# Two attention stages of a transformer block: VectorE put into source order in the second, and the weight-sum matmuls issued one step later in the first

## The chip, the cores and the metric

The kernel runs on one core of a Trainium2 chip. The metric is the device time of one execution in microseconds (us); smaller is better. A core has TensorE (PE, matrix products, with a separate weight load PEld), VectorE (DVE), ScalarE (ACT), GpSimd (POOL) and SyncE (SP, which issues most of the DMAs). Each engine executes its own list of instructions in order; engines wait for each other by semaphores.

## The reference, cut to what matters

The input has 4 batches of 512 tokens and 512 channels. Four sublayers follow each other, each with a layer norm in front and a residual sum behind it.

```python
x = x + attn0(layernorm(x))        # 16 heads of 32, rope, rms norm of q and k, causal softmax
x = x + ternary_ffn(layernorm(x))
x = x + selective_scan(layernorm(x))
z = layernorm(x)
h = z + attn1(rmsnorm(z, ln1))     # latent attention, 16 heads of 32, causal softmax
x = x + h + moe(rmsnorm(h, ln2))   # one shared and seven routed experts, top 2
```

Both attentions compute `softmax(q k^T * scale, causal) v` and then a product with an output matrix. In both the sum of the exponentials is divided out only after the product with `v`.

## The kernel before, in words

Tiles have 128 partitions. In both attentions PSUM is divided into two pair buffers, each of two banks (`pair`), and four single banks (`bank`). All names of tiles that come from `pair` share the two buffers (`sc`, `scd`, `pqd`), and all that come from `bank` share the four (`sm`, `av`, `pq`, `tp`, `tpd`, `avd`, `y`, `pl`, ...).

**Order.** The instructions are written in Python loops, and a scheduler (Tile's) then places the instructions of each engine by a model of their durations. `tc.manual_schedule(engines=...)` (L417 and L1457 here) takes the named engines out of this: they keep the order in which the source issues them. In before that is TensorE alone, in both attentions; VectorE, ScalarE, GpSimd and SyncE are placed by the scheduler. It may therefore draw an instruction forward past others of its engine if its inputs are there.

**First attention** (`attend`, L346). For each batch there are 16 steps (g, j): 4 groups of 4 heads, 4 blocks of 128 keys. Scores are kept transposed, with keys on the partitions, so the weights need no transposing, but the sums over keys need a matmul with ones. A step consists of
- `scores` (L361 to L367): 4 matmuls into two `sc` pairs, 2 exponentials on ScalarE into `pt`, and a causal mask on GpSimd (`affine_select`),
- `add` (L385): VectorE adds the weights of the block before to those of this one, so that one matmul with ones gives the running sum,
- `weigh` (L377): 4 matmuls of the weights with `v` into the bank `av`,
- `invert` (L392, L396): 8 matmul instructions with ones into the bank `sm` (the sums of 128 queries, 4 heads), a reciprocal on VectorE, and after the last block the product `oT` (L398).

At loop index m the source issues the scores of step m, the `add` of step m-2, then the fillers `between[m]` (projections of the next batch L284, the output product of the last one L340, transposes, jobs for the ternary weights), then `weigh` of step m-1, then `invert` of step m-2. After the loop two transposes of the next batch follow (`turn_heads`), and then `finish`, which in before adds and inverts the last step.

**Second attention** (L1457 to L1487). One loop over 128 steps plus 4, 32 steps for each batch: 4 head groups, 4 blocks t of 128 queries, 2 pairs of heads. Within a batch, `at` is the number of the step, and this document calls it step 0 to 31. At step m the source issues
- `turn` of step m-3: transposes of the weights on TensorE (L1410) into `tpd`, copied to `ptd` once by VectorE (L1415) and once by ScalarE (L1417),
- `soften` of step m: the scores `scd` (L1387, 4 rows of the array in use), on VectorE the addition of the mask (L1390) and the negative maximum `nm` (L1395), on ScalarE two exponentials `pr` (L1398) with their sums,
- at the ends of groups `widen_sums` (L1441, L1443) and `invert` (L1453, L1455), and in every second step `weigh` (L1428) for two pairs four steps back, with the product `oTd` (L1435) at a group's end,
- as fillers from step 4 a part of `leave(b-1)`: four output products `y` (L1327) with residual sums (L1330, L1331) and squares (L1335) in steps 4 to 7, scaling (L1342) and transposes into `hTr` in steps 8 to 11, then the router,
- and from step 7 a part of `enter(b+1)` (from L1002): statistics of the layer norm (L108, L109) in steps 7 to 10; at step 11 the shift (L150), and in steps 11 to 14 the normalised rows (L155, ScalarE) and their squares (L1015, ScalarE); the inverse root (`ri_rms`: L102 on VectorE, the power L103 on GpSimd) at step 14; from step 15 scaled rows `row_d` (L1028) and their transposes into `hTd` (L132, L133); then the latent projections (L1044, L1062 to L1069) and the rotations.

`enter` for batch 1 runs in batch 0, and so on; batch 3 has none. `leave` for batch 0 runs in batch 1, and so on. The input `x` of all batches is there when the second attention begins.

These are the loops of the two stages around the edit, as the printed functions show in full:

```python
if m > 1:
    add(*steps[m - 2])
for part in between.get(m, ()):
    part()
if m > 0:
    weigh(*steps[m - 1])
if m > 1:
    invert(*steps[m - 2])
```

Of the kernel before, what the change touches and what calls it, by code (L numbers as in the profile page):

```python
# [46 lines left out]
def block_kernel(ctx: ExitStack, tc: tile.TileContext, a: dict, out: bass.AP):  # L47
# [16 lines left out]
    def pair(name):  # L64
        return banks["pair"].tile([P, 2, 512], F32, tag="pair", name=name)

    def bank(name):
        return banks["bank"].tile([P, 512], F32, tag="bank", name=name)
# [95 lines left out]
    with tc.tile_pool(name="a_w", bufs=1) as aw, tc.tile_pool(name="a_1", bufs=1) as a1, tc.tile_pool(  # L164
# [180 lines left out]
        def attend(b, between):  # L345

            qkT, v = turned_qk[b], values[b]
            oT = outs[b] = a1.tile([P, NK, T], F32, tag="oT", name="oT")
            weights, averages, inverses = {}, {}, {}

            def scores(g, j):
                w = T - j * P
                pt = weights[g, j] = a2.tile([P, HG, w], F32, tag=f"pt{j}", name=f"pt{j}", bufs=1)
                both = [pair("sc") for _ in range(2)]
                for i in range(HG):
                    rows = slice(i * D, (i + 1) * D)  # L360
                    nc.tensor.matmul(  # L361
                        both[i // 2][:, i % 2, :w], qkT[rows, NG + g, j * P : (j + 1) * P],
                        qkT[rows, g, j * P :], start=True, stop=True,
                    )
                for i, sc in enumerate(both):
                    nc.scalar.activation(pt[:, 2 * i : 2 * i + 2, :w], sc[:, :, :w], AF.Exp, scale=SCALE)  # L366
                nc.gpsimd.affine_select(  # L367
                    out=pt[:, :, 0:P], in_=pt[:, :, 0:P], compare_op=ALU.is_ge, fill=0.0,
                    base=0, pattern=[[0, HG], [1, P]], channel_multiplier=-1,
                )  # L370

            def weigh(g, j):
                if j == 0:
                    averages[g] = bank("av")
                for i in range(HG):
                    h = g * HG + i
                    nc.tensor.matmul(  # L377
                        averages[g][i * D : (i + 1) * D, j * P :], v[:, j, h * D : (h + 1) * D],
                        weights[g, j][:, i, :], start=j == 0, stop=j == NT - 1,
                    )  # L380

            def add(g, j):
                if j > 0:
                    pt = weights[g, j]
                    nc.vector.tensor_tensor(pt, pt, weights[g, j - 1][:, :, P:], ALU.add)  # L385

            def invert(g, j):
                if j == 0:
                    inverses[g] = a2.tile([P, T], F32, tag="r", name="r", bufs=1)
                sm = bank("sm")  # L390
                for i in range(HG):
                    nc.tensor.matmul(  # L392
                        sm[i * D : (i + 1) * D, :P], ones[:, :D], weights[g, j][:, i, :P],
                        start=True, stop=True,
                    )
                nc.vector.reciprocal(inverses[g][:, j * P : (j + 1) * P], sm[:, :P])  # L396
                if j == NT - 1:
                    nc.vector.tensor_tensor(oT[:, g, :], averages.pop(g), inverses.pop(g), ALU.mult)  # L398

            steps = [(g, j) for g in range(NG) for j in range(NT)]  # L400
            for m in range(len(steps) + 1):
                if m < len(steps):
                    scores(*steps[m])
                if m > 1:
                    add(*steps[m - 2])
                for part in between.get(m, ()):
                    part()
                if m > 0:
                    weigh(*steps[m - 1])
                if m > 1:  # L410
                    invert(*steps[m - 2])
            return lambda: (add(*steps[-1]), invert(*steps[-1]))

        def do(f, *args):
            return lambda: f(*args)
# [1 line left out]
        with tc.manual_schedule(engines={mybir.EngineType.PE}):  # L417
# [39 lines left out]
            for b in range(B):  # L457
# [20 lines left out]
                if b == B - 1:  # L478
                    first_mv = const.tile([P, NT, 2], F32, tag="mv", name="mv")
                    for t in range(NT):  # L480
                        between[9].append(do(statistics, a1, xs[0], t, first_mv))
                finish = attend(b, between)
                if b + 1 < B:
                    turn_heads(b + 1, 2)
# [302 lines left out]
    with tc.tile_pool(name="b_s", bufs=1) as bs, tc.tile_pool(name="b_1", bufs=1) as b1, tc.tile_pool(  # L787
# [79 lines left out]
        with tc.manual_schedule(engines={mybir.EngineType.PE}):  # L867
# [4 lines left out]
            for b in range(B):  # L872
# [10 lines left out]
                def part(n):  # L883
                    if n % 3 == 2 and n > 3 * 4 and b + 1 < B:
                        next(coming, None)
                        if not light[0]:
                            return
                    if n not in (2, 3, 5):
                        light[0] = next(between, False)
# [194 lines left out]
    with tc.tile_pool(name="c_1", bufs=1, reuse_waits="tile") as c1, tc.tile_pool(  # L1084
# [7 lines left out]
        steps = [(b, n, half) for b in range(B) for n in range(NS) for half in range(2)]  # L1092
# [19 lines left out]
        def turn(b, n, half, i):  # L1112
            bu = bank("bu")
            k = 2 * half + i

            nc.tensor.matmul(  # L1116
                bu[:, :P], loaded[b][1][:, 0, k * P : (k + 1) * P], scaled[b, n][0],
                start=True, stop=True,
            )
            for t in range(1, NT):  # L1120
                nc.tensor.transpose(  # L1121
                    bu[:, t * P : (t + 1) * P], scaled[b, n][t][:, k * P : (k + 1) * P], ident
                )
            turned.setdefault((b, n, half), []).append(bu)
# [9 lines left out]
        def weigh(b, n, half):  # L1134
            if half == 0:
                cb = c1.tile([P, T], F32, tag="cb", name="cb", bufs=3)
                nc.sync.dma_start(cb, c_rows[b, n].partition_broadcast(P))
                weighed[b, n] = cb
            hc = c2.tile([P, 2, T], F32, tag="hc", name="hc", bufs=4)
            nc.gpsimd.tensor_tensor(  # L1140
                hc, states.pop((b, n, half)), weighed[b, n].unsqueeze(1).to_broadcast([P, 2, T]), ALU.mult
            )
            states[b, n, half] = hc
# [23 lines left out]
        engines = {getattr(mybir.EngineType, e) for e in ("PE", "DVE", "Activation", "Pool", "SP")}  # L1167
# [142 lines left out]
    with tc.tile_pool(name="d_1", bufs=1) as d1, tc.tile_pool(name="d_2", bufs=2) as d2, tc.tile_pool(  # L1310
# [128 lines left out]
        def widen_sums(b, g):  # L1439
            total = sums.pop((b, g))  # L1440
            nc.vector.reciprocal(total, total)  # L1441
            wides[b, g] = d1.tile([P, T], F32, tag="wide", name="wide")
            nc.scalar.copy(  # L1443
                wides[b, g].rearrange("p (t i d) -> p t i d", t=NT, i=HG),
                total.unsqueeze(3).to_broadcast([P, NT, HG, D]),
            )

        def invert(b, g):

            wide = wides.pop((b, g))  # L1450
            tp = bank("tpr")
            for t in range(NT):
                nc.tensor.transpose(tp[:, t * P : (t + 1) * P], wide[:, t * P : (t + 1) * P], ident)  # L1453
            inverses[b, g] = d1.tile([P, T], F32, tag="inv", name="inv")
            nc.scalar.copy(inverses[b, g], tp)  # L1455

        with tc.manual_schedule(engines={mybir.EngineType.PE}):  # L1457
            for _ in come:
                pass
            left = iter(())  # L1460
            n = len(pairs)
            each = n // B
            for m in range(n + 4):
                b, at = divmod(m, each)
                if 3 <= m < n + 3:
                    turn(*pairs[m - 3])
                if m < n:
                    soften(*pairs[m])
                if 1 <= m < n + 1 and pairs[m - 1][2:] == (NT - 1, 1):
                    widen_sums(*pairs[m - 1][:2])  # L1470
                if 3 <= m < n + 3 and pairs[m - 3][2:] == (NT - 1, 1):
                    invert(*pairs[m - 3][:2])
                if m >= 5 and m % 2 == 1:
                    weigh(*pairs[m - 4][:3])

                if m == (B - 1) * each:
                    fetch_shared()
                if m >= each and at == 3:
                    left = leave(b - 1, outs[b - 1])
                if at >= 4:  # L1480
                    next(left, None)
                if at == 7:
                    come = enter(b + 1, d2) if b + 1 < B else iter(())
                if at >= 7:
                    next(come, None)

            filler = shared(0, d1, "lat")  # L1487
            for _ in range(NK):
                next(filler)
            for _ in range(NT):  # L1490
                next(left)
            for _ in filler:
                pass
            for _ in left:
                pass
# [6 lines left out]
    with tc.tile_pool(name="e_1", bufs=1, reuse_waits="tile") as e1, tc.tile_pool(  # L1502
# [255 lines left out]
        engines = {mybir.EngineType.PE, mybir.EngineType.DVE, mybir.EngineType.Activation}  # L1758
# [64 lines left out]
```

## Time and profile before

| | us |
|---|---|
| median of 3 runs | 1857.02 |
| lowest and highest | 1854.37, 1859.17 |
| the profiled execution | 1858.7 |
| its span, first to last instruction | 1857.0 |
| first attention with its projections | about 55 to 424 of the span |
| ternary feed-forward | 424 to about 740 |
| selective scan | about 740 to 1102 |
| second attention | about 1102 to 1512 |
| experts | 1512 to 1857 |

The mean clock granted to TensorE is 0.98 of full speed. All times of instructions that follow are microseconds from the start of the span of this one profiled execution.

How to read the lines. A row of a stretch has its start and end, its length, then for PE, PEld, DVE, ACT and POOL the busy time and in brackets the number of instructions, then the granted TensorE clock, the share of the DMA engines' time and GB/s (a row asked for TensorE alone has only its busy time in front of the clock). A row of waits reads "engine, tile and line that waited <- engine, tile and line that released it: us in total, times, longest". A row of the timeline has the start, the duration, the engine, line, operation, the tile written and those read, the shapes, the number of instructions drawn together, and in square brackets the idle time of the engine just before it with what ended it.

### The profile page before, as it was taken

What the parts mean: (1) busy time and instruction counts of PE and PEld (TensorE: products, weight loads), DVE (VectorE), ACT (ScalarE), POOL (GpSimd) and SP (SyncE); (2) the same over time, 40 slices, a digit from 0 to 9 for tenths busy, and PEclk for the clock granted to TensorE, in tenths of its full rate; (3) what the DMA queues carried; (4) which work ended last, traced back from release to release, by engine and by line L of the source; (5) the groups of instructions that cost most, each with busy time, mean ns of one, the idle gap of its engine ahead of it and who ended that gap; (6) DMA issues with size and microseconds to landing.
All of it is one profiled execution on the core that took longest, in us unless ns stands there. A gap on an engine that the chain in (4) does not pass through costs nothing.

```text
span 1857.0 us, 27575 instructions
## 1 busy us (share of the span) xinstructions
PE 1740.2 (94%) x10374; PEld 1093.0 (59%) x10374; DVE 1186.6 (64%) x1908; ACT 938.0 (51%) x1940; POOL 581.5 (31%) x383
## 2 busy tenths in 40 slices
PE   7899899989999998989997989999999999999998
PEld 3443344437777676878886875556556554544444
DVE  6577757786655556899887886574766764322222
ACT  2433533332242536889988867576676652111111
POOL 2231313120202021889887860100000000244431
PEclk9999999999999999999999988999999999999999
DMA  7002300102011112333223200000010006455545
GB/s 244 22 1 68 109 1 1 46 1 76 5 40 53 59 56 82 94 92 102 58 73 102 58 28 1 1 24 1 1 35 24 24 24 230 150 91 91 91 79 142
DMA packets 74630, 115.07 MB, mean 62 GB/s; under 512 B 9546, under 2 KB 34762, under 8 KB 73940
## 3 DMA queue, kind: packets, MB, share of 16 engines
q1 hardware_dynamic: 64996, 90.87, 15.4%
q0 software_dynamic: 8656, 20.32, 6.1%
q10 hardware_dynamic: 848, 2.13, 0.3%
q8 instruction: 83, 1.36, 0.3%
q14 instruction: 47, 0.39, 0.1%
HBM read 83.02 MB, written 33.42 MB: 63 GB/s over the span
## 4 chain that ended last, share of the span: by engine, by line
PE 68%; DVE 13%; ACT 11%; issue 3%; DMA 3%; POOL 1%; DVEq 0%; SPq 0%; ACTq 0%; POOLq 0%
PE pgr L1702 7%; PE pg L844 6%; PE pq L284 5%; PE ys L1153 4%; PE yr L1723 4%; PE scd L1387 4%; PE bu L1121 3%; PE y L1327 3%; PE y L862 3%; PE pge L1288 3%; PE tp L132 3%; PE bu L1116 3%; PE y L340 3%; PE tpd L1410 2%; ACT pr L1398 2%
## 5 line engine op out<-in xcount | busy, mean ns | idle before, releaser
L1140 POOL TENSOR_TENSOR hc<-h,cb 128x1024 f32<-128x1024 f32 x128 | 301.1, 2378 | 115.4 <-DVE h L1129 93.7
L1129 DVE TENSOR_TENSOR_SCAN h<-da,bu 128x512 f32<-128x512 f32 x256 | 295.1, 1204 | 28.5 <-PE bu L1121 14.3
L284 PE MATMUL pq<-wqkv,hT 128*128 128x512 f32 x384 | 179.6, 615 | 4.8 <-DVE qk L300 3.6
L1109 ACT ACTIVATE da<-delta_l,am 128x511 f32<-128x511 f32 x256 | 163.4, 709 | 2.1 <-DVE h L1129 2.0
L1398 ACT ACTIVATE pr<-scd,nm 128x128 f32<-128x128 f32 (+3 forms) x256 | 133.3, 530 | 57.6 <-DVE nm L1395 56.7
L844 PE MATMUL pg<-hTh,w 128*128 128x512 f32 (+1 forms) x352 | 145.6, 414 | 1.0 <-ACT hTh L831 0.7
L844 PE MATMUL pg<-hTl,w 128*128 128x512 f32 (+1 forms) x352 | 139.9, 397 | 0.2 <-DVE hTl L832 0.2
L1153 PE MATMUL ys<-ident,hc 128*128 128x128 f32 x1024 | 136.7, 277 | 3.3 <-DVE h L1129 1.7
L1121 PE MATMUL bu<-ident,bu 128*128 128x128 f32 x768 | 132.2, 279 | 6.4 <-ACT bu L1103 6.4
L1702 PE MATMUL pgr<-wgu,gTe 128*128 x304 | 137.1, 593 | 0.0
L1103 ACT ACTIVATE bu<-dxT,bts 128x512 f32<-128x512 f32 x192 | 124.3, 712 | 16.2 <-PE bu L1121 13.3
L284 PEld LDWEIGHTS pq<-wqkv,hT 128*128 128x128 f32 x384 | 71.5, 194 | 97.3 <-issue 91.2
L366 ACT ACTIVATE pt<-sc 128x1024 f32<-128x1024 f32 (+3 forms) x128 | 83.3, 698 | 78.0 <-PE sc L361 72.3
L1387 PE MATMUL scd<-kTd,qTd 32*128 32x512 f32 (+3 forms) x512 | 109.0, 507 | 14.0 <-ACT pr L1398 11.3
L1153 PEld LDWEIGHTS ys<-ident,hc 128*128 128x128 f32 x1024 | 119.0, 143 | 4.3 <-DVE h L1129 1.9
L1116 PE MATMUL bu<-diag_l,dxT 128*128 128x128 f32 x512 | 105.9, 289 | 16.3 <-DVE h L1129 13.3
L367 POOL TENSOR_SCALAR_AFFINE_SELECT pt<-pt 128x512 f32<-128x512 f32 x64 | 56.2, 879 | 179.1 <-ACT pt L366 156.5
L1395 DVE TENSOR_REDUCE nm<-scd 128x2 f32<-128x256 f32 (+3 forms) x128 | 105.0, 821 | 2.8
L1410 PE MATMUL tpd<-ident,pr 128*128 128x128 f32 x640 | 102.6, 290 | 3.5 <-ACT ptd L1417 1.1
L1116 PEld LDWEIGHTS bu<-diag_l,dxT 128*128 128x128 f32 x512 | 82.3, 196 | 40.0 <-DVE h L1129 23.2
L1121 PEld LDWEIGHTS bu<-ident,bu 128*128 128x128 f32 x768 | 95.6, 145 | 9.9 <-ACT bu L1103 9.9
L1709 DVE SCALAR_TENSOR_TENSOR hidr<-pgr,silr 128x256 f32<-128x256 f32 x38 | 16.1, 425 | 130.0 <-ACT silr L1707 130.0
(338 smaller groups left out, 3290.7 us busy)
## 6 DMA issues: line engine op xcount, KB each, us to landing
cb<-c_rows SPq DMA_DIRECT2D x64, 256.0 KB, 3.3
q_w<-in_w2T SPq DMA_DIRECT2D x20, 256.0 KB, 2.8
diag_l<-diags SPq DMA_DIRECT2D x64, 64.0 KB, 2.0
hrows<-h SPq DMA_DIRECT2D x4, 1024.0 KB, 4.3
acc<-x SPq DMA_DIRECT2D x16, 256.0 KB, 2.0
wgu<-in_r_gate SPq DMA_DIRECT2D x7, 512.0 KB, 9.5
wgu<-in_r_up SPq DMA_DIRECT2D x7, 512.0 KB, 10.0
wdn<-in_r_down SPq DMA_DIRECT2D x7, 512.0 KB, 9.3
```

Source lines behind the costliest of these rows:

```text
L284: nc.tensor.matmul(y, inputs_T[b][:, k, t * P : (t + 1) * P], wqkv[:, k, s * C : (s + 1) * C], start=k == 0, stop=k == NK - 1,)
L844: nc.tensor.matmul(pg[:rows, i, :], w[:, k, f * P : f * P + rows], part[:, k, :], start=k + m == 0, stop=k + m == NK,)
L1109: nc.scalar.activation(da[:, k, 1:], delta[:, k, 1:], AF.Exp, scale=am[:, k, n : n + 1])
L1116: nc.tensor.matmul(bu[:, :P], loaded[b][1][:, 0, k * P : (k + 1) * P], scaled[b, n][0], start=True, stop=True,)
L1121: nc.tensor.transpose(bu[:, t * P : (t + 1) * P], scaled[b, n][t][:, k * P : (k + 1) * P], ident)
L1129: nc.vector.tensor_tensor_scan(h[:, i, :], decays[b, n][:, 2 * half + i, :], bu, 0.0, ALU.mult, ALU.add)
L1140: nc.gpsimd.tensor_tensor(hc, states.pop((b, n, half)), weighed[b, n].unsqueeze(1).to_broadcast([P, 2, T]), ALU.mult)
L1153: nc.tensor.matmul(sums[b][t][:, k * P : (k + 1) * P], hc[:, i, t * P : (t + 1) * P], ident, is_transpose=True, start=n == 0 and k == 0, s ...
L1387: nc.tensor.matmul(sc[:, i, :w], qT[at, g, t * P : w], kT[at, g, :w], start=True, stop=True)
L1398: nc.scalar.activation(pr[:, i, :w], sc[:, i, :w], AF.Exp, bias=nm[:, i : i + 1], accum_out=sums[b, g][:, t, 2 * p + i : 2 * p + i + 1],)
L1410: nc.tensor.transpose(tp[:, j * P : (j + 1) * P], pr[:, i, j * P : (j + 1) * P], ident)
L1702: nc.tensor.matmul(pg, gT[:, k, :], wgu[:, bass.ds(e, 1), k, :].rearrange("p e o -> p (e o)"), start=k == 0, stop=k == NK - 1,)
```

## The change

In the first attention `invert` is issued for step m-3 instead of m-2, and ahead of the fillers and of `weigh`, directly behind `add`. The last `add` and the last but one `invert` move from `finish` into `attend`, so that they come ahead of the two `turn_heads`; `finish` keeps the last `invert`. On TensorE the `sm` matmuls of a step thereby stand behind the next step's scores instead of in front of them. In the second attention VectorE joins TensorE in the order of the source. No instruction is added, removed or resized on any engine.

```diff
                 if m > 1:
                     add(*steps[m - 2])
+                if m > 2:
+                    invert(*steps[m - 3])
                 for part in between.get(m, ()):
                     part()
                 if m > 0:
                     weigh(*steps[m - 1])
-                if m > 1:
-                    invert(*steps[m - 2])
-            return lambda: (add(*steps[-1]), invert(*steps[-1]))
+            add(*steps[-1])
+            invert(*steps[-2])
+            return lambda: invert(*steps[-1])
...
-        with tc.manual_schedule(engines={mybir.EngineType.PE}):
+        with tc.manual_schedule(engines={mybir.EngineType.PE, mybir.EngineType.DVE}):
```

In the built programs the engines compare as follows. TensorE's list differs in the first attention alone: 52 groups of `sm` change places with the next `sc`. VectorE's differs throughout the second attention: the maximum `nm` stands directly behind the addition of the mask in every step, the copy `ptd` after it, and the parts of `enter` and `leave` stand in the step that issues them. ScalarE's list, placed by the scheduler, changes with it: in batches 0 to 2, L155 and L1015 stand four times each in steps 11 to 14, with two `row_d` and the first `hTd` copy behind the last of them and in front of step 15's exponentials. In before, the rows L155 for batches 1 to 3 had been placed at 1111.7 to 1216.3, in batch 0 and the first steps of batch 1, and the squares L1015 in the first steps of batch 0 and in steps 7 and 8 of batches 1 and 2. On GpSimd four powers for `ri_ln` come later; on SyncE one store of `hrows` (1 MB) is issued behind four loads of `acc`.

## The prediction

> **What bounds the kernel now.** First the page: busy times and the chain of work that ended last.
>
> ```profile
> PE 1740.2 (94%) x10374; PEld 1093.0 (59%) x10374; DVE 1186.6 (64%) x1908; ACT 938.0 (51%) x1940; POOL 581.5 (31%) x383
> PE 68%; DVE 13%; ACT 11%; issue 3%; DMA 3%; POOL 1%; DVEq 0%; SPq 0%; ACTq 0%; POOLq 0%
> ```
>
> TensorE bounds it, so an edit that leaves TensorE's instructions alone is worth the TensorE idle time that it removes or adds, and the clock that goes with it. Next the busy time by stage: the first attention stands in 55 to 405, the second in 1102 to 1512, two of its full batches in these rows (first figures: length, then TensorE busy).
>
> ```profile
> 1210.00:1320.00 110.00, 105.12 (x824) 63.11 (x823) 69.50 (x143) 74.73 (x223) 7.14 (x6) 1.00 0.03 11
> 1320.00:1430.00 110.00, 105.17 (x826) 63.32 (x825) 69.61 (x143) 72.33 (x220) 7.12 (x6) 1.00 0.08 25
> ```
>
> A batch has 4.9 us of TensorE idle in 110. VectorE (69.5) and ScalarE (74.7) have room on average, so only the order in which they serve TensorE counts. Then the waits of TensorE, in 55 to 405 (first line) and in 1110 to 1512 (the others):
>
> ```profile
> PE sm L392 <- DVE pt L385: 11.1, 13, 1.9
> ...
> PE scd L1387 <- ACT pr L1398: 8.8, 15, 1.5
> PE pqd L1066 <- ACT pr L1398: 2.5, 3, 0.9
> ```
>
> These are what the change can win: 11.1 us and 8.8 to 11.3 us.
>
> **Part 1, first attention.** Nothing is added or removed; 52 groups of eight `sm` matmuls (0.42 us a group) trade places with the next step's `sc` matmuls (L361). The timeline of TensorE shows the best case:
>
> ```profile
> 173.95 0.42 PE L392 MATMUL sm<-pt,ones 128*32 128x128 f32 x8 [1.94 <-DVE pt L385]
> 174.31 1.14 PE L361 MATMUL sc<-qkT 32*128 32x512 f32 x8
> ```
>
> Here the 1.14 us of scores move in front and run under the wait: 1.1 gained. The 13 waits, one by one in the timeline: six (0.90 and 0.62 at the end of batches 0, 1 and 2) have no scores left to move, so nothing: 4.56 us stay. Two (0.54 and 0.55, VectorE held by rotations of the projection) vanish: 1.1. Four (0.90, 0.97, 0.90, 0.73; 3.5 us) are in steps with no projection beside them, where the next scores wait for an exponential in turn; I take 0.8. The 1.94 at 405.82 is the tail, whose `add` now comes before the last inversion: 0.5. Sum 1.1 + 1.1 + 0.8 + 0.5 = **-3.5 us**. Bounds: all 6.5 movable us at one end; at the other +2, because the `sm` bank and the `av` bank are released later by a step and the projections (615 ns a matmul) draw from the same four; I found no user of a bank that comes within 3.7 us of its release, so I stay near the gain.
>
> **Part 2, second attention.** VectorE now keeps the order of the source; TensorE's order is unchanged there, POOL has four small `ri_ln` powers (1.0 us each) later, SP issues one 1 MB `hrows` store behind four `acc` loads (landing 2 to 4.3 us, nobody in this stage waits for them). ScalarE has the same instructions but is placed anew around VectorE.
>
> *Gain.* In before the copy of a turned block often slips between the mask add and the maximum of the next scores:
>
> ```profile
> 1308.73 0.43 DVE L1390 TENSOR_TENSOR scd<-scd,neg 128x256 f32<-128x256 f32 x1 [0.27 <-PE scd L1387]
> 1309.07 0.41 DVE L1415 COPY ptd<-tpd 128x256 f32<-128x256 f32 x1
> 1309.40 0.95 DVE L1395 TENSOR_REDUCE nm<-scd 128x2 f32<-128x768 f32 x1
> ```
>
> In source order the maximum is first, so the exponential and the two-buffered `scd` behind it come 0.33 us earlier. 15 waits of TensorE are on that: at most 15 x 0.33 = 5 us, at least 0 where the copy, now 0.8 us later, holds a `tpd` bank instead. I take **-3.5**, nearer the gain because the banks' row (`tpd` <- DVE `ptd`) shows no TensorE wait now. At the ramp two statistics (1.28 us) no longer stand before the first mask add: **-1.5**, between 0 and the 2.43 us wait for `pr` at 1105.88.
>
> *Loss.* `enter(b+1)` and `leave(b-1)` share VectorE's order. In before the scheduler drew `enter` forward: the 12 normalisations (L155) run from 1111.7 to 1216.3, long before their steps, the squares (L1015) at steps 7 to 8 of a batch. In the new order the shift (L150) stays at step 11, and ScalarE, which waits for it, gets 4 L155 and 4 L1015, both `row_d` (L1028) and the first `hTd` copy at steps 11 to 14, in front of the exponential of step 15. The same stretch of before in batch 1, ScalarE then TensorE:
>
> ```profile
> 1253.23 0.69 ACT L1398 ACTIVATE pr<-scd,nm 128x512 f32<-128x512 f32 x1 [0.18 <-DVE nm L1395]
> ...
> 1256.17 0.68 ACT L1398 ACTIVATE pr<-scd,nm 128x512 f32<-128x512 f32 x1
> 1256.74 0.20 ACT L1398 ACTIVATION_READ_ACCUMULATOR pr<-scd,nm 128x1 f32 x1
> ```
>
> ```profile
> 1256.99 0.49 PE L1387 MATMUL scd<-kTd,qTd 32*128 32x128 f32 x4
> ```
>
> The scores of step 17 start 0.05 us after the exponential of step 15, whose buffer they need: TensorE has no slack here, and what ScalarE is late is lost one for one. From start to start, one L155 takes 0.72, a square with its read 0.62, a `row_d` 0.62, the copy 0.49. Batches 1 and 2 get 4 x 0.72 + 4 x 0.62 + 0.62 + 0.49 = 6.5 us more in the stretch, and 1.1 us in which `row_d` waits for the POOL power (the row of before at 1244.99 has 1.14). To cover it there are ScalarE's idle pieces between 1246 and 1257 (0.42, 0.64, 0.18, 0.33: 1.6) and 1.0 because one `row_d` with its wait leaves the front: 6.5 + 1.1 - 1.6 - 1.0 = 5.0 each. Batch 0 had four L155 there already: 2.5 + 2 x 0.62 + 0.5 + 1.1 = 5.3, less 2.3 of idle (0.98 and 1.36): 3.0. Batch 3 has no `enter`. Sum **+13 us**; bounds 0 (ScalarE catches up in its 26.0 us of waits for `tpd` before TensorE notices) and 20 (no cover at all). I take the worked middle because of the 0.05 us.
>
> *Clock.* A stall has a tail in this trace. Granted clock is the figure after the busy times:
>
> ```profile
> 1134.00:1138.00 4.00, 2.49 (x21) 1.00 0.00 0
> 1138.00:1142.00 4.00, 4.00 (x30) 0.69 0.02 4
> 1142.00:1146.00 4.00, 4.00 (x22) 0.50 0.00 0
> ```
>
> A wait of 1.51 us at 1137.40 is followed by 6.8 us at half clock, worth 3.4. The stretch 143 to 147 was as empty (2.45 of 4) and was not followed by one. So the new stalls in batches 1 and 2 bring it in one of two: **+3.4**, bounds 0 and 10.
>
> The Trainium skill, "TensorE: Matmul & The Clock Gate", section "What's actually happening", has the array go slow only after an idle window of about 3.4 us and fast after one busy window. This trace differs in both: half clock after a 1.51 us wait, and from 1106 to 1126 seven such windows at 0.50 with TensorE shown busy. By the page the stalls here would cost no clock, and the sum would be 3.4 us lower.
>
> **Sum.** The profiled execution took 1858.7 us (span 1857.0), 1.7 over the median of the runs. 1858.7 - 3.5 - 3.5 - 1.5 + 13 + 3.4 = 1866.6; less 1.7 on the median's scale, **1865 us**, about 0.4% slower.
>
> **Rivals.**
> - *ScalarE's lump is absorbed, faster.* Mechanism: the exponentials get ahead by the earlier maxima, so the steps 11 to 14 eat a lead and not TensorE's time. It decides where a batch's lead exceeds 5 us; against it stands the two-deep `scd`, which allows a lead of one step (2.5 us), for it the 45.2 us that ScalarE spends waiting for `nm`. 1858.7 - 8.5 - 1.7 = 1848.5.
> - *Gains and losses cancel.* Half the lump (6.5), no clock: 1855; with all of it and no clock 1861.5. Within 0.3%, which is about what a measurement of this kernel can tell from no change.
> - *Every stall costs the clock, and VectorE blocks too.* `ri_rms` (L102) at step 14 waits on VectorE for ScalarE's fourth square, and the copy, mask and maximum of step 15 queue behind it, so lateness feeds itself: 1865 + 2 x 3.4 for the clock = 1872, and 1878 with the uncovered lump.
>
> **Chances.** Forecast 0.42, absorbed 0.22, cancel 0.20, more clock 0.16. So slower by over 0.3% 0.58, within 0.20, faster 0.22. The range 1848 to 1878 leaves out about half of the absorbed case and little above. The forecast's own range is 1861 to 1870.
>
> **What would show it.** Right: a batch (110 us now) grows by about 5; TensorE waits for `pr` at steps 15 to 17 grow from nothing to some 5 us a batch; L155 runs at steps 11 to 14 in every batch; `sm` <- `pt` falls from 11.1 to about 7. Wrong: no wait there, batches of 107 to 109 us; or the ramp's half clock (1102 to 1126) changing length, which I cost at nothing but which moves the end by 1.7 us for each 3.4 us window; or bank waits on `tpd` from `ptd`.

## The result, and the profile after

The changed kernel takes 1882.83 us (median of 4 runs, 1880.0 to 1885.8) where the kernel before takes 1856.95 in the same comparison. The ratio is 1.0134 (95% interval 1.0117 to 1.0151): slower by about 26 us. The prediction had the sign, but its 1865 and its range up to 1878 were too low.

The first line of the page shows the same work. TensorE is shown busy 18 us longer with as many instructions:

```profile
PE 1758.6 (93%) x10374; PEld 1095.1 (58%) x10374; DVE 1183.6 (63%) x1908; ACT 940.0 (50%) x1940; POOL 585.4 (31%) x383
```

Where the 26.9 us of span came in is read from the same instruction in both timelines (before, after, difference):

| instruction | before | after | later by |
|---|---|---|---|
| first `pg`, behind the first attention | 428.25 | 434.77 | 6.5 |
| first `scd`, start of the second attention | 1102.63 | 1110.64 | 8.0 |
| last `tpr` of batch 0 | 1210.87 | 1220.64 | 9.8 |
| last `tpr` of batch 1 | 1321.24 | 1338.36 | 17.1 |
| last `tpr` of batch 2 | 1431.43 | 1457.32 | 25.9 |
| last `tpr` of batch 3 | 1510.20 | 1535.69 | 25.5 |
| `found`, in the router behind it | 1582.64 | 1610.32 | 27.7 |

So the first attention lost 6.5 and the second 17.5, nearly all of it in batches 1 and 2 (110.4 and 110.2 us from one last `tpr` to the next before, 117.7 and 119.0 after). Two stages between them, which the change doesn't touch, differ by 1.5 in these two executions; over all kept profiles the way from the first `pg` to the first `scd` takes 671 to 679, and the six kernels with the first attention of before reach `pg` at 422.1 to 428.3. So a difference of one execution from another is good to a few us; medians and profiles of several kernels decide below.

The waits of TensorE in the first attention of the changed kernel, in 55 to 430:

```profile
PE sm L392 <- DVE pt L385: 8.8, 9, 1.8
PE sc L361 <- ACT pt L366: 7.5, 10, 1.8
PE pq L284 <- DVE qk L300: 5.1, 3, 3.3
```

In before (55 to 424) these were 13.2, 4.2 and 3.6, and all waits of 0.15 us and more together 28.3; now they are 25.2. **The waits did shrink by 3.1 us, and the stage still became longer.** That loss is in no row of waits.

The waits of TensorE in the second attention, 1110 to 1540 (line numbers are 2 higher than before):

```profile
PE scd L1389 <- ACT pr L1400: 10.4, 17, 2.5
PE tpd L1412 <- ACT ptd L1419: 4.5, 9, 1.0
...
PE tp L132 <- DVE shift L150: 2.2, 2, 1.1
...
PE tpd L1412 <- ACT hTd L133: 2.1, 3, 0.7
PE tp L132 <- ACT row_d L1030: 1.8, 3, 0.7
PE tpd L1412 <- ACT hTr L133: 1.4, 2, 0.7
```

The wait for `pr`, which the prediction expected to grow, did not: with the ramp in both windows it was 11.3 us (16 times) in before, from 1102 on, and is 10.4 (17 times) now. New or longer are waits for `ptd`, `hTd`, `row_d`: copies and rows on ScalarE. From one last `tpr` to the next, in batch 1 and again in batch 2, the waits grew from 4.7 to 9.6 us: those that ScalarE ended from 3.6 to 7.7, those that VectorE ended (`shift` and `h`) from 1.1 to 2.0. ScalarE's timeline in batch 1, steps 14 and 15, shows what stands in its list there:

```profile
1264.21 0.85 ACT L155 ACTIVATE h<-x,shift,ri_ln 128x512 f32<-128x512 f32 x1
1264.93 0.40 ACT L1419 COPY ptd<-tpd 128x256 f32<-128x256 f32 x1
1265.18 0.67 ACT L1017 ACTIVATE sq_d<-h 128x512 f32<-128x512 f32 x1
...
1265.81 0.84 ACT L155 ACTIVATE h<-x,shift,ri_ln 128x512 f32<-128x512 f32 x1
1266.51 0.71 ACT L1400 ACTIVATE pr<-scd,nm 128x512 f32<-128x512 f32 x1
...
1267.84 0.67 ACT L1017 ACTIVATE sq_d<-h 128x512 f32<-128x512 f32 x1
1268.36 0.24 ACT L1017 ACTIVATION_READ_ACCUMULATOR sq_d<-h 128x1 f32 x1
1268.45 0.51 ACT L1419 COPY ptd<-tpd 128x384 f32<-128x384 f32 x1
1269.92 1.33 ACT L1030 ACTIVATE row_d<-h,ri_rms 128x512 f32<-128x512 f32 x2 [0.96 <-POOL ri_rms L103]
1271.38 0.60 ACT L133 ACTIVATE hTd<-tp 128x512 f32<-128x512 f32 x1
1271.88 0.68 ACT L1400 ACTIVATE pr<-scd,nm 128x512 f32<-128x512 f32 x1
```

ScalarE has no idle time until it waits 0.96 us for the root in front of `row_d`, and both the copies of turned weights and the exponentials stand behind the rows and squares of the next batch. TensorE answers there:

```profile
1269.02 0.55 PE L1412 MATMUL tpd<-ident,pr 128*128 128x128 f32 x3 [0.98 <-ACT ptd L1419]
...
1270.69 0.55 PE L132 MATMUL tp<-ident,row_d 128*128 128x128 f32 x3 [0.71 <-ACT row_d L1030]
...
1272.04 1.51 PE L1412 MATMUL tpd<-ident,pr 128*128 128x128 f32 x8 [0.69 <-ACT hTd L133]
```

The last one has a duration of 1.51 where the same eight had 1.09 at 1250.24: the granted clock fell. It fell after the stalls of batch 1 and of batch 2 (0.83 in 1270 to 1280; 0.93 and 0.73 in 1380 to 1400).

### The profile page after: what moved, and what is told of

Same layout as the page of the kernel before. It is cut to its first block, busy times and chain, and to the rows that moved or that the text cites. A ratio compares the mean times of both kernels' runs of the same rounds, so it can differ in the third digit from the quotient of the medians.

```text
span 1883.9 us, 27551 instructions
## 1 busy us (share of the span) xinstructions
PE 1758.6 (93%) x10374; PEld 1095.1 (58%) x10374; DVE 1183.6 (63%) x1908; ACT 940.0 (50%) x1940; POOL 585.4 (31%) x383
## 5 line engine op out<-in xcount | busy, mean ns | idle before, releaser
L1389 PE MATMUL scd<-kTd,qTd 32*128 32x512 f32 (+3 forms) x512 | 110.0, 509 | 12.9 <-ACT pr L1400 10.4
L1412 PEld LDWEIGHTS tpd<-ident,pr 128*128 128x128 f32 x640 | 75.9, 148 | 47.3 <-issue 17.6
L103 POOL TENSOR_TENSOR ri_ln<-ri_ln,minus_half 128x4 f32<-128x4 f32 (+1 forms) x17 | 16.9, 994 | 276.9 <-DVE ri_ln L102 241.0
L367 POOL TENSOR_SCALAR_AFFINE_SELECT pt<-pt 128x512 f32<-128x512 f32 x64 | 49.5, 774 | 170.0 <-ACT pt L366 146.6
## 6 DMA issues: line engine op xcount, KB each, us to landing
wgu<-in_r_up SPq DMA_DIRECT2D x7, 512.0 KB, 10.1
```

Of the source, the lines that this page charges most:

```text
L1389: nc.tensor.matmul(sc[:, i, :w], qT[at, g, t * P : w], kT[at, g, :w], start=True, stop=True)
L1412: nc.tensor.transpose(tp[:, j * P : (j + 1) * P], pr[:, i, j * P : (j + 1) * P], ident)
```

## The experiments

Each is compared with the kernel before on the same chip. "Faster" and "slower" are against that kernel.

**1. The two parts alone.** First the edit of the first attention without the other, then the other alone (the two halves of the diff of the change).

> The edit of the first attention alone; the second attention as before. Theory A (the sums lose their place behind the values' matmuls, and each of the 52 moved groups costs 0.14 us more, worked out from the distances of the groups in the two traces): 52 x 0.14 = 7.3 us of TensorE, less some 2 to 4 us of waits, so 4 to 7 us slower than before, with sm<-pt waits near 5 and first attention 6 us longer. Theory B (the step of the prediction: only waits go): 3 to 4 us faster, and all of the change's 26 us belong to the second attention.

> VectorE in source order in the second attention alone; first attention as before. Theory A: 17 to 21 us slower than before (17.5 in the second attention of the changed kernel, 1.7 behind it). Theory B: all 26 us.

The first attention alone is 5.5 us slower (1861.77 against 1856.26; ratio 1.0032, 1.0019 to 1.0045); `sm`'s waits for `pt` stay at 8.8 there, not near 5 as theory A had it. VectorE alone is 20.8 slower (1877.09; 1.0118, 1.009 to 1.0145). Together that is 26.3, the whole change. The step of the prediction that gave the first attention a gain (theory B) falls.

Why does it lose while its waits shrink? The distances of the groups in the timeline, in a step that waits for nothing: before, and the changed kernel.

```profile
283.79 0.43 PE L377 MATMUL av<-pt,v 128*32 128x128 f32 x8
284.03 0.40 PE L392 MATMUL sm<-pt,ones 128*32 128x128 f32 x8
284.36 0.93 PE L361 MATMUL sc<-qkT 32*128 32x384 f32 x8
285.22 1.12 PE L284 MATMUL pq<-wqkv,hT 128*128 128x512 f32 x2
```

```profile
291.25 0.43 PE L377 MATMUL av<-pt,v 128*32 128x128 f32 x8
291.61 0.93 PE L361 MATMUL sc<-qkT 32*128 32x384 f32 x8
292.46 0.43 PE L392 MATMUL sm<-pt,ones 128*32 128x128 f32 x8
292.82 1.55 PE L284 MATMUL pq<-wqkv,hT 128*128 128x512 f32 x3
```

From `av` to `pq` it is 1.43 in before and 1.57 after, with the same three groups. The 0.12 stands at `av`: the next group comes 0.24 us after it where that is `sm`, of the same form (128 rows by 32 columns), and 0.36 where it is `sc`; the rest is at `sm` (0.33 and 0.36). 52 x 0.14 = 7.3 us, at most, as a group that waits anyway pays nothing; the waits of this kernel fall by 2.0 (28.3 to 26.3).

The traces hold another loss that no row of waits shows. The scores of a step need two `sc` buffers; where the second comes free later than the first, the eight instructions run in two halves, one behind the other. The same step in before and in the changed kernel:

```profile
305.47 0.93 PE L361 MATMUL sc<-qkT 32*128 32x384 f32 x8
```

```profile
313.74 1.83 PE L361 MATMUL sc<-qkT 32*128 32x384 f32 x8 [0.40 <-ACT pt L366]
```

The row shows a wait of 0.40, and the scores take 0.90 longer besides. Summed over the 64 steps, without the waits themselves, such lengthening is 9.9 and 10.1 us in the two kernels with the change's order, and 4.9 to 6.2 in the six with that of before: some 4 us more. 7.3 + 4 - 2.0 = 9.3 is more than the 5.5 measured (3.5 to 8.4 by the interval), so how the loss divides between neighbours and halved scores stays open.

**2. The sums late, but next to `av`.** If the neighbour costs the time, the later step can be had without it. In `e3_late_adjacent` the inversion follows `weigh`, in `e4_late_in_front` it precedes it (the diff is that of the first, against the changed kernel):

```diff
-                if m > 2:
-                    invert(*steps[m - 3])
                 for part in between.get(m, ()):
                     part()
                 if m > 0:
                     weigh(*steps[m - 1])
+                if m > 2:
+                    invert(*steps[m - 3])
```

> First attention alone: the sums one step later as in the change, but issued behind weigh, so that sm still follows av on TensorE as in before. Theory A (the neighbours on TensorE cost the time, the later step wins its waits): no 7.3 us, the sm<-pt waits fall to some 3 or less, so 3 to 8 us faster than before. Rival (issuing the sums a step later costs by itself, since banks and weights come free later): slower than before by 3 to 7, like the change's own first attention.

> As the run before, but the sums directly in front of weigh instead of directly behind it, so sm and av are neighbours again, in the other order. Theory A: same saving of about 0.14 us a group as with sm behind av, so 3 to 8 us faster than before and within 3 us of the run before. Rival (only sm behind av overlaps): 4 us slower to 1 faster than before.

Behind `weigh`: 1.7 faster (1854.60; 0.9993, 0.998 to 1.0006), which holds zero. In front of it: 2.6 slower (1858.88; 1.0012, 0.9999 to 1.0025), which holds it too. That lies in the range of its rival (only `sm` behind `av` overlaps), but the timeline doesn't bear the rival out: `av` starts 0.24 after `sm` there, and the next `sc` 0.33 after `av`. From the first `sc` to the first `pg` it takes 361.3 us, among the 358.8 to 363.1 of the kernels with the order of before, and in batch 3 of the second attention, which it doesn't touch, its profile has a stretch of 10.2 us at half clock at 1500. The sums are as late as in the change or later by half a step, so the rival (lateness costs) falls; the distance is 1.43 again, here in the run with the sums behind `weigh`:

```profile
282.12 0.43 PE L377 MATMUL av<-pt,v 128*32 128x128 f32 x8
282.36 0.40 PE L392 MATMUL sm<-pt,ones 128*32 128x128 f32 x8
282.69 0.93 PE L361 MATMUL sc<-qkT 32*128 32x384 f32 x8
283.55 0.70 PE L284 MATMUL pq<-wqkv,hT 128*128 128x512 f32 x1
```

The expected 3 to 8 us of gain did not come in either. It was run once more:

> The sums late and behind weigh, alone, once more: its waits fell by 3.7 us in the profile, its time by 1.7 with an interval that holds zero. If the waits are worth their length, 2 to 4 us faster than before; if the clock eats them, within 1.5 of before.

1856.24 against 1856.40 (1.0004, 0.9991 to 1.0018): no difference. `sm` <- `pt` fell from 13.2 to 2.4, but waits for `oT`, `r`, `qk` and `pq` came up, the sum of all fell from 28.3 to 25.1, and of the rest the time shows nothing. Four kept profiles have this order (this run twice, and the runs of 5 and 6), and two things in them work against the gain. The halved scores add 6.6 to 8.0 us, where the order of before has 4.9 to 6.2. And from the first `sc` to the first `pg` the half clock costs 13.7 to 15.4 us, against 7.0 to 12.0 in the six with the order of before. Over all executions of the two runs, though, the mean clock of the whole kernel is 0.978 and 0.977, as good as the 0.978 of before, so that the clock took the gain isn't shown.

**3. Two breaks instead of one.** The sums between the two halves of the next scores, by a call inside `scores` between heads 1 and 2.

> First attention alone, second as before: the change's order, but the sums of step m-3 stand between the two halves of the scores of step m (after heads 0 and 1), so TensorE changes the form of its matmuls twice more a step than in before instead of once. Theory A (each further change of form costs 0.14 us): 2 x 7.3 less 2 to 3 of waits, 11 to 14 us slower than before. Rival (a late sum costs by itself, its neighbours don't matter): 4 to 7 slower, like the change's first attention alone (5.5).

1880.01, that is 23.8 us slower (1.0122, 1.0094 to 1.0149): neither theory. The timeline says why, and it is a fault of the experiment:

```profile
289.36 0.49 PE L363 MATMUL sc<-qkT 32*128 32x128 f32 x4
289.78 0.43 PE L394 MATMUL sm<-pt,ones 128*32 128x128 f32 x8
290.13 0.49 PE L363 MATMUL sc<-qkT 32*128 32x128 f32 x4
290.55 3.70 PE L340 MATMUL y<-wo,oT 128*128 128x512 f32 x8
```

Half of the scores (x4) takes 0.42 us, as long as all eight did (0.44 at 281.20 of the changed kernel): the four heads use different rows of the array at the same time, and the split ended that. The doubled scores are about 37 us (0.42, 0.63, 0.84 and 1.06 by width, 52 steps), and some 6 us of them were paid in before already, where scores ran in two halves; with the 7.3 of the neighbours, and less 11.8 us of waits (28.3 to 16.5), that is about 26, where 23.8 were measured. `sm` takes 0.35 here with `sc` on both sides, as in the changed kernel. So theory A in its wide form, a price for each change of form, has no support; what stands is the narrow one: `av` and `sm` side by side save some 0.14 us a step.

**4. The second attention: is it ScalarE's lump or VectorE's order?** VectorE stays in source order in all of these; TensorE's order doesn't change in the first.

```diff
-                if at == 7:
+                if at == 0:
                     come = enter(b + 1, d2) if b + 1 < B else iter(())
-                if at >= 7:
+                if at < 8 or at >= 15:
                     next(come, None)
```

> VectorE in source order in the second attention, first attention as before; enter's statistics, normalised rows and squares are issued in steps 0 to 7 of a batch instead of 7 to 14, the rest of enter from step 15 as it was. TensorE's order is the same as with VectorE in order alone (20.8 us slower than before). Theory L (ScalarE's lump at steps 11 to 14 costs it): 12 us or more come back, 0 to 8 slower than before; batches 1 and 2 near 110 us. Rival D (VectorE's source order costs by itself, with copies late and banks held): the waits stay, 14 to 20 slower.

1860.61 against 1858.02, 2.6 us slower by the medians (1.0016, 1.0002 to 1.0031): 18 of the 20.8 us are gone. Both batches take 111.7 us from one last `tpr` to the next. TensorE's waits in such a batch (1222 to 1340 of this run), the first three:

```profile
PE tpd L1410 <- ACT ptd L1417: 2.4, 3, 1.3
PE scd L1387 <- ACT pr L1398: 1.4, 4, 0.6
PE tp L132 <- ACT qTd L133: 0.7, 1, 0.7
```

None for `row_d`, `shift` or `hTr` any more, and for `hTd` one of 0.3. Rival D falls: with the normalisation early, VectorE's order costs 2.6 us (0.4 to 5.8 by the interval). The loss belongs to where the next batch's normalisation stands. The edit moves VectorE's part of it (statistics and shift) with ScalarE's (rows and squares); that ScalarE's part is what costs rests on the waits, four fifths of which ScalarE ended, and on the runs that follow.

Next, what in the lump costs: two ways of thinning it.

> VectorE in source order in the second attention, first attention as before; the root of the sums of squares (ri_rms) is issued one step later, at step 15, so that the two row_d and the first hTd copy can't stand in front of step 15's exponentials. The amount of ScalarE's work in steps 11 to 15 stays nearly the same. Theory L by placing (a chain squares, root, power, row_d, hTd in front of step 15): 6 to 10 of the 20.8 us come back, 10 to 15 slower than before. Theory L by amount (8 eighths of rows and squares in four steps): 0 to 3 come back, 18 to 21 slower.

```diff
-            if t == NT - 1:
-                rs = root_inverse(pool, ss, RMS_EPS, 1.0 / C, "rms")
             yield
+        rs = root_inverse(pool, ss, RMS_EPS, 1.0 / C, "rms")
```

1877.20, 21 us slower (1.0109, 1.0087 to 1.0131): nothing came back that can be measured, and 10 to 15 lies below the interval; "by amount" had 18 to 21. The stall at `ptd` shrank (4.8 with VectorE alone in order, 2.8 here) and the one at the rows took its place:

```profile
PE tp L132 <- ACT row_d L1027: 5.9, 3, 2.6
PE tpd L1409 <- ACT ptd L1416: 2.8, 8, 0.5
```

TensorE's transposes of `row_d` keep their place and now wait 2.6 us at a time. So the run moved the stall; it doesn't tell whether the place of `row_d` and `hTd` in front of step 15 is a cause.

> VectorE in source order in the second attention, first attention as before; the normalised rows (L155) of batches 1 to 3 are made by GpSimd instead of ScalarE, at their old steps. ScalarE has 4 x 0.72 = 2.9 us less in steps 11 to 14 of three batches. Theory L, one for one: 6 to 9 us come back, 12 to 15 slower than before. Rival D: nothing comes back, 19 to 22 slower; or more, where GpSimd's rows come so late that the squares and ri_rms wait for them.

The edit is a `gpsimd.tensor_scalar` (subtract the mean, multiply by the root) in place of `shifted`. 1891.30, that is 33.3 slower (1.0189, 1.0172 to 1.0206): worse, by the last clause of what was expected. A row takes 2.07 us on GpSimd, four follow each other (8.24 us), and the squares wait for them in ScalarE's list:

```profile
ACT sq_d L1020 <- POOL h L1014: 15.4, 12, 3.2
```

ScalarE does 8.7 us less and stands still for 15.4 more, with copies and exponentials behind the standing square. What counts is how long ScalarE's list is held up at these steps, by work or by waiting.

> TensorE, VectorE and ScalarE in source order in the second attention, first attention as before; enter at its old steps. The lump's amount is the same, but ScalarE no longer has two row_d and the first hTd copy in front of step 15's exponentials. Theory L by amount: 14 to 20 us slower than before. Theory L by placing (most of the loss is what stands in front of step 15): 2 to 10 slower. Rival (ScalarE needs the freedom elsewhere): over 25 slower.

1915.00, 57 us slower (1.0298, 1.0273 to 1.0324): none of the theories on the lump, the rival. In source order an exponential waits for its maximum with the copies behind it:

```profile
ACT pr L1398 <- DVE nm L1395: 117.4, 79, 2.9
```

With the scheduler's placing (experiment with `enter` early) that row is 60.0, 67 times. ScalarE needs the scheduler's freedom more than VectorE does; the run says nothing on the lump's place.

**5. The clock at the start of the second attention.** The prediction cost the half clock of 1102 to 1126 at nothing. Can it be kept up? Matmuls without a reader, on top of `e3_late_adjacent`:

```diff
+                if m in (0, 2):
+                    warm = bank("warm")
+                    for _ in range(4):
+                        nc.tensor.matmul(warm, ident, xs[0][:, 0, :], start=True, stop=True)
                 if m < n:
                     soften(*pairs[m])
```

> The sums late and behind weigh (1.7 us faster than before in its own run), second attention scheduled as before, and eight matmuls whose result nobody reads (0.59 us each): four ahead of the first scores of the second attention and four behind the second, where TensorE waits 2.3 and 2.4 us. If these waits are what lets the clock fall to half from 1102 to 1126, the clock stays up and up to 12 us come back: 8 to 13 us faster than before. If the clock falls for another reason: 2 slower to 2 faster.

1859.45, 3.3 slower (1.0022, 1.0011 to 1.0033). The clock came up and fell again, after a wait of 2.20 us at 1112.68 (busy time and clock of TensorE):

```profile
1108.00:1112.00 4.00, 2.48 (x14) 1.00 0.01 2
1112.00:1116.00 4.00, 3.32 (x20) 0.76 0.00 0
1116.00:1120.00 4.00, 3.28 (x16) 0.50 0.00 0
1120.00:1124.00 4.00, 4.00 (x20) 0.50 0.00 0
```

The fill shortened the half clock: from 1100 on it lasts 20.5 us here (1100.4 to 1103.9 and 1114.1 to 1131.2), and 34.1 in both profiles of the late sums without the fill and with the second attention of before; the difference is worth 6.8 us. But it cost as much: the eight matmuls, two instructions each, took 5.3 us ahead of the first scores, partly at half clock, and 3.6 behind them, where 2.4 were idle. Nothing was left of it in the time. The question of whether a full cover would keep the clock up was not tried.

**6. Both mended.** The sums late behind `weigh`, and `enter` early:

> The whole change with its two losses mended: the sums one step later but behind weigh, VectorE in source order in the second attention, and enter's statistics, rows and squares in steps 0 to 7. If the two causes are all there is and they add up, -1.7 and +3.0: 0 to 4 us slower than before, that is 22 or more of the change's 26 us come back. If something else of the change costs, over 6 slower.

1859.92 against 1856.40, 3.5 slower (1.0018, 1.0003 to 1.0033). Of the change's 26 us 22 are gone, so the two causes are nearly all of it. No version beat the kernel before by more than the noise.

## Why the prediction was wrong, point by point

- **First attention, -3.5.** This step failed, in its words "Nothing is added or removed; 52 groups of eight `sm` matmuls (0.42 us a group) trade places", costed by waits alone. The waits of the stage fell by 3.1, near the 3.5 worked out; but a traded place costs up to 0.14 us, 7.3 in all, and the halved scores some 4. The rows of before already held the first: from an `av` of 512 columns it is 0.88 us to `sm` (86.64 to 87.52), and 1.00 to `sc` in the four steps that have no `sm` between (70.82 to 71.82). Measured alone: +5.5. Nine of the missing 18 us are here.
- **Earlier maxima, -3.5, and the ramp, -1.5.** Too large. In after the waits of TensorE for `pr` in steps without fillers are 0.55, 0.16 and 0.55 where they were 0.75, 0.56 and 0.21: 0.26 a stretch, less than 2 us in all. At the ramp the 2.43 became 2.52: nothing.
- **The lump, +13.** The mechanism was right, and nearly the size: steps 8 to 17 added 2.2 us in batch 0, and 7.7 and 9.2 in batches 1 and 2, clock included. Without the 1.7 and 3.4 of half clock that is 14.0. The place was wrong, so that the size came so near is partly luck: not the exponential of step 15 and the scores of step 17, but the copies `ptd` and the banks behind them from step 14 on, and waits for `h`, `hTr` and `shift` from step 8.
- **Clock, +3.4.** It fell in both batches, 1.7 and 3.4, so +5.1. (The seven windows at 0.50 that the prediction counts from 1106 to 1126 are those from 1102 to 1126; TensorE is shown busy in nearly all of the time from 1106 on, 19.95 of 20 us, but not in the first.)
- **Behind the second attention, 0.** Not seen: `leave` of batch 3 runs on after the loop, and there VectorE's order lets the transposes wait 1.44 us for the scaled rows (L1344); the router came 2.2 later.
- **Rivals.** The absorbed lump and the cancelling one fell with the 7 to 9 us in each of batches 1 and 2. "More clock" had the right neighbourhood (1872 to 1878) for a partly wrong reason: VectorE did block on `ri_rms` (2.73 us at 1268.63), but moving that root a step later moved the stall to `row_d` and gave nothing measurable back.

The new sum, from the profiled execution: 1858.7 + 6.5 (first attention) + 17.5 (second) + 2.2 (behind it) + 1.5 (stages not touched), less 0.7 in the experts, is 1885.7; that execution took 1885.8.

## What to carry to other kernels

A reorder on the bounding engine has a price of its own: before counting waits, measure in the timeline how far apart the neighbours start now, and what they would start after. A short wait can cost more than its row says where it parts instructions that would run together. And when one engine's order is fixed, look at what the scheduler then does to the engines that were filled with its forerunners' work: most of the new waits were for ScalarE, and most of the loss went by issuing that work seven steps earlier.

## What the runs showed of the hardware

- Two groups of column-tiled matmuls of one form (128 rows by 32 columns) follow each other more closely: at 128 columns the second starts 0.24 us after the first, where scores (32 rows by 128 columns) start after 0.36.
- Four heads of scores on 32 rows each run together: half of them takes 0.42 us, all 0.44. Where the buffer of the second pair comes late they run in two halves, 1.83 us in place of 0.93 at 384 columns.
- TensorE at half clock stays there: 24 us from 1102 to 1126 in before, and from 1114 to 1131 in the run with the extra matmuls, with TensorE shown busy most of that time; stalls of 0.7 to 1.1 us close together were enough to start a shorter one (7 us or less) in batches 1 and 2. The Trainium skill, "TensorE: Matmul & The Clock Gate", section "What's actually happening", has the clock come back after about 3.4 us of sustained work; these runs show it later, and why isn't settled here.
- One row of 128 x 512 in float32 with two per-partition operands takes 2.07 us on GpSimd and 0.82 on ScalarE.
